# Leaving the second softmax of a gated slot attention undivided, and repairing it in the epsilon of the normalization

## The chip, the core and the metric

The kernel runs on one core of one Trainium2 chip. The metric is the device time of one execution in microseconds (us). A core has five engines that run their own instruction queues in order: PE (TensorE, matrix products; its weight loads are listed as PEld), DVE (VectorE), ACT (ScalarE), POOL (GpSimd) and SP (SyncE, which issues the DMAs). They wait for each other by semaphores.

## The reference

Input is x of 2 x 2048 x 512 in f32. One layer of gated slot attention with 16 heads, then a feed-forward layer with a Hadamard transform; each is followed by a residual sum and a layer norm. Of the attention, what matters here:

```
q, k (64 per head), v, g (128 per head), s (64 slots per head, clipped) = x @ weights
ok_t[m] = sum over u <= t of (q_t . k_u) * weight of token u in slot m      # M = 64 slots
p       = softmax(ok, over the 64 slots)
o_t     = sum over m of p_t[m] * (slot m's running mean of v up to t)
o       = o * rsqrt(mean(o*o over 128) + 1e-5) * g_norm_weight
o       = o * silu(g);   y = o @ Wo
```

The weights of the tokens in a slot are exp(s), divided by their running sum z. So ok is a causal product divided by z, and the same division by z is needed a second time when p meets the values.

If p is left as e = exp(ok - max), with S the sum of e over the slots, then o becomes S * o. The normalization gives the same result if its epsilon is multiplied by S*S, since S*o / sqrt(mean((S*o)^2) + S*S*eps) = o / sqrt(mean(o^2) + eps).

## The kernel before, in words

The heads go in four groups (g) of four; the 2048 tokens in 16 chunks (n) of 128, both batch rows at once. A `Step` is one group on one chunk: 64 steps, group by group. Its tiles hold the 128 tokens in the partitions and NQ = 4 pairs of columns of heads, eight (head, batch) pairs in all; `HALVES` are the two halves of 64 partitions, in which slots and state of two batch rows or heads lie.

`run` (called once per step) writes out by hand the order of the instructions of three steps in flight: `now` (projections, scores, the slots' softmax), `before` (the step one earlier: values, normalization, output products) and `old` (two earlier: the rest of the output products, rows stored). The order of PE, DVE, ACT and POOL is the order in which `run` calls the methods; nothing is moved by a scheduler there. DMAs are issued by SP.

All large products are made by seven products of quarter blocks (Strassen's scheme in Winograd's form): `q`, `v` and `o` with k = 1 to 7, whose sums lie in the PSUM tags c1 (two buffers), c2 and c3. `Unit.into` brings a product from PSUM to SBUF, on ACT (lines 458 and 460) or on DVE (463). PE's lines: 503 for q, k and s; 529 for values and gates; 746 for the output product, which reads the tile `ob`; its results are added to the rows on DVE (742).

The steps that the change and the prediction speak of, in the order of one `run`:

- PE's `state_values` (687) ends the values `po` of `before`. `gated` then squares them on ACT (704, three instructions because half of the partitions change sides), multiplies them by the gate on DVE (706), sums the squares on DVE (708), and on POOL scales and adds epsilon (710), raises to the power -0.5 (711) and multiplies (713).
- `softmax` of `now` on DVE: division by z (625), the maximum (631), its subtraction (633); the exponential on ACT (634).
- `softmax_sum`: sum over the slots (638) and its reciprocal (639) on DVE; the second multiplication by 1/z on POOL (640).
- `o_transposed` of `before`: eight transposes on PE (730) of what 713 made; `right_factor` copies them into `ob` on ACT (427, 428) and makes further parts on DVE (432, 433) and POOL (434, 435).
- `softmax_end` of `now`: the multiplication of r by 1/S on DVE (644).
- product 4 of `v`, copied by ACT (460); the tanh on ACT (539); products 1, 5 and 2 of `o` (746) with their additions (742) and, between them, the gate's last step on DVE (543). Then the next `run` begins with product 1 of `q` (503), product 3 of `o` and product 2 of `q`.
- r, made in this run, is read by the next run's `r_transposed` on PE (649), after product 6 of `q`.

The tile pool `small` has four buffers of each name, among them `sm`, which holds S.

```
do(now, "softmax_sum")
if o_last:
    nw["o"].sums(2)
    nw["o"].sums(3, nc.gpsimd)
do(before, "o_transposed")
do(now, "softmax_end")
main("v", 4)
```

Of the kernel before, what the change touches and what calls it, by code (L numbers as in the profile page):

```python
# [9 lines left out]
F32 = mybir.dt.float32  # L10
AF = mybir.ActivationFunctionType
ALU = mybir.AluOpType
AX = mybir.AxisListType
PSUM = bass.MemoryType.PSUM

P = 128
# [4 lines left out]
DV = 128  # L21
M = 64
HG = 4
NG = H // HG
NQ = 4
TH = P // 2
HALVES = (slice(0, TH), slice(TH, P))
# [6 lines left out]
EPS = 1e-5  # L34
# [4 lines left out]
def gated_slot_attention_ffn_kernel(  # L39
# [13 lines left out]
    nc = tc.nc  # L53
# [7 lines left out]
    small = ctx.enter_context(tc.tile_pool(name="small", bufs=4))  # L61
# [86 lines left out]
    xb, acc, res, h, wt = {}, {}, {}, {}, []  # L148
# [203 lines left out]
    with ExitStack() as att:  # L352
# [34 lines left out]

        QUARTERS = [(i, j, HALVES[j], s, HALVES[s], HALVES[s ^ j]) for i in range(NQ) for j in range(2) for s in range(2)]
        OPENS = (1, 2, 5)

        def settle(sums):

            nc.scalar.copy(small.tile([P, 1], F32, name="seen", bufs=1), sums)
# [71 lines left out]
        class Step:  # L465
# [31 lines left out]
            def multiply_q(self, out, k):  # L497
                wt = w["qks"].t
                for c in range(2):
                    xk, wk_ = self.xb[:, RIGHT[k], c, :], wt[:, LEFT[k], c, :]  # L500
                    for i in range(3):
                        a, b = (wk_[:, i * P : (i + 1) * P], xk) if i < 2 else (xk, wk_[:, 2 * P :])
                        nc.tensor.matmul(  # L503
                            out[:, i * P : (i + 1) * P], lhsT=a, rhs=b,
                            start=(k in OPENS and c == 0 and i == 0), stop=(c == 1), skip_group_check=True,
                        )
# [20 lines left out]
            def multiply_v(self, out, k):  # L527
                for c in range(2):
                    nc.tensor.matmul(  # L529
                        out, lhsT=self.xb[:, RIGHT[k], c, :], rhs=w["vg"].t[:, LEFT[k], c, :],  # L530
                        start=(k in OPENS and c == 0), stop=(c == 1), skip_group_check=True,
                    )
# [101 lines left out]
                nc.scalar.activation(r, r, AF.Exp, scale=DK**-0.5)  # L634

            def softmax_sum(self):
                self.sm = small.tile([P, 2 * NQ], F32, name="sm")
                nc.vector.tensor_reduce(self.sm, self.r8, AX.X, ALU.add)
                nc.vector.reciprocal(self.sm, self.sm)
                nc.gpsimd.tensor_tensor(self.r, self.r, self.iz, ALU.mult)  # L640

            def softmax_end(self):
                smb = self.sm.rearrange("p (h o) -> p h o", o=1).to_broadcast([P, 2 * NQ, M])
                nc.vector.tensor_tensor(self.r8, self.r8, smb, ALU.mult)


            def r_transposed(self):
# [48 lines left out]
            def gated(self):  # L696

                sq = c1.tile([P, 2, NQ, DV], F32, name="sq", tag="big")
                self.gj = self.t2[:, :, HD:].rearrange("p q (j d) -> p j q d", d=DV)

                every = slice(0, P)
                moves = [(0, every, every), (1, HALVES[0], HALVES[1]), (1, HALVES[1], HALVES[0])]
                for j, to, at in moves:
                    nc.scalar.activation(sq[to, j], self.po[j][at], AF.Square)  # L704
                for j, to, at in moves:
                    nc.vector.tensor_tensor(self.gj[to, j], self.po[j][at], self.gj[to, j], ALU.mult)  # L706
                ss = small.tile([P, 2 * NQ], F32, name="ss")
                nc.vector.tensor_reduce(ss, sq.rearrange("p j q d -> p (j q) d"), AX.X, ALU.add)  # L708
                self.state()
                nc.gpsimd.tensor_scalar(ss, ss, 1.0 / DV, EPS, ALU.mult, ALU.add)  # L710
                nc.gpsimd.tensor_tensor(ss, ss, mhalf, ALU.pow)
                ssb = ss.rearrange("p (j q o) -> p j q o", j=2, o=1).to_broadcast([P, 2, NQ, DV])
                nc.gpsimd.tensor_tensor(self.gj, self.gj, ssb, ALU.mult)
# [30 lines left out]
            def multiply_o(self, out, k):  # L744
                for c in range(2):
                    nc.tensor.matmul(  # L746
                        out, lhsT=self.ob[:, RIGHT[k], c, :], rhs=w["o"].t[:, LEFT[k], c, :],
                        start=(k in OPENS and c == 0), stop=(c == 1), skip_group_check=True,
                    )
# [248 lines left out]
        def run(new, now, before, old):  # L998


            def do(step, name, *args):
                if step is not None:
                    getattr(step, name)(*args)

            def main(name, k):

                if now is not None:
                    getattr(now, name)(k)
                elif before is not None:
                    for _ in range(FILL[name, k]):  # L1010
                        next(ups)
# [120 lines left out]
                nw["o"].sums(2)  # L1132
                nw["o"].sums(3, nc.gpsimd)
            do(before, "o_transposed")
            do(now, "softmax_end")
            main("v", 4)
            if last:
                nw["vg"] = load_vg(g + 1)
# [23 lines left out]
        with tc.manual_schedule(  # L1162
            engines={mybir.EngineType.PE, mybir.EngineType.DVE, mybir.EngineType.Activation, mybir.EngineType.Pool}
        ):
            steps[0].load_x()
            nw["qks"] = load_qks(0)
            steps[1].load_x()
            nw["vg"] = load_vg(0)
            nw["o"] = load_o(0)
            steps[0].make_x()  # L1170
            for k in range(4):
                nw["qks"].sums(k)
            N = len(steps)
            for i in range(N + 2):
                if i == N:
                    open_x("wvg", OUTER[3:], 4 * P)
                    open_acc("ux", tag="h1")
                    ups = up(0, h)
                run(*(steps[j] if 0 <= j < N else None for j in (i + 1, i, i - 1, i - 2)))
            for _ in pieces[0]:  # L1180
                pass
# [6 lines left out]
    with tc.manual_schedule(  # L1188
# [11 lines left out]
        for u in range(NU):  # L1200
            if u:
                h = {}
# [89 lines left out]
```

## Time and profile before

| | us |
|---|---|
| three runs | 3512.81, 3513.03, 3518.43; median 3513.03 |
| profiled execution, span from its first to its last instruction | 3516.1 (granted TensorE clock 0.999) |
| attention part, 0 to 2430 us: busy PE / DVE / ACT / POOL | 2388.6 / 1656.9 / 815.8 / 630.1 |
| rest, 2430 to 3516 us: busy PE / DVE / ACT / POOL | 1068.1 / 698.0 / 141.2 / 514.1 |
| line 639, 64 instructions on DVE | 13.0 (203 ns each) |
| line 644, 64 instructions on DVE | 77.9 (1217 ns each) |
| line 710, 64 instructions on POOL | 12.7 (198 ns each) |

The profile is of one execution; no time of its own is given for it beside its span, which is 3.1 us above the median of the three runs. A busy PE is not the same as PE at its peak, since the ends of matmuls are modelled; its starts are better guides. A line of the timeline gives start, length, engine, line of the code, what is written and read, and in brackets the idle time of that engine just before and who ended it.

### The profile page before, as it was taken

Reading aid. Unit: us, or ns where it says so; the run is one execution under the profiler, and the core shown is the slowest. Engines: PE = TensorE matmul, PEld = TensorE weight load, DVE = VectorE, ACT = ScalarE, POOL = GpSimd, SP = SyncE. Lnnn points to the kernel's source line nnn. Section 1 sums busy time; section 2 is a strip of 40 time slices with the busy share of each in tenths; the row PEclk is TensorE's granted clock in tenths of the full one; section 3 lists DMA queues with packets and bytes.
Section 4 is the critical chain, followed back from the end, with each engine's and each line's share of the span. In section 5 each row is a group of like instructions: output and inputs, shape, how many; then the busy total and the mean of one; then the engine's idle time right before and its main releaser. Section 6 shows DMA issues by size and latency. Waiting matters only on the chain. (4 is left out here: it accounts for less than half of the span.)

```text
span 3516.1 us, 75258 instructions
## 1 busy us (share of the span) xinstructions
PE 3456.7 (98%) x31840; PEld 2702.8 (77%) x31840; DVE 2354.9 (67%) x3940; ACT 957.0 (27%) x1712; POOL 1144.2 (33%) x1069
## 2 busy tenths in 40 slices
PE   8999999999999999999999999998999999999998
PEld 6777777677777677677777777776888888888887
DVE  5777776665666765656766677777666756756756
ACT  3333333333333333333333333332111111111110
POOL 1222223221221331221332222223634643643544
PEclk9999999999999999999999999999999999999999
DMA  5334334221122232122222243347555544445431
GB/s 184 118 113 138 118 119 152 93 72 62 55 66 70 94 96 65 52 66 70 74 99 68 69 140 129 102 160 270 171 179 205 174 161 176 156 151 184 163 135 68
DMA packets 208833, 425.03 MB, mean 121 GB/s; under 512 B 19696, under 2 KB 120432, under 8 KB 207472
## 3 DMA queue, kind: packets, MB, share of 16 engines
q1 hardware_dynamic: 208496, 420.22, 35.7%
q8 instruction: 250, 4.10, 0.5%
q14 instruction: 87, 0.71, 0.1%
HBM read 297.47 MB, written 125.30 MB: 120 GB/s over the span
## 5 line engine op out<-in xcount | busy, mean ns | idle before, releaser
L529 PE MATMUL c<-wvg,xb 128*128 128x512 f32 x1792 | 812.7, 598 | 4.0 <-DVE wvg L412 2.0
L529 PEld LDWEIGHTS c<-wvg,xb 128*128 128x128 f32 x1792 | 322.1, 190 | 369.6 <-issue 291.9
L503 PE MATMUL c<-xb,wqks 128*128 128x128 f32 x3584 | 553.2, 277 | 15.7 <-DMA wqks<-wqks_blocks 9.6
L503 PEld LDWEIGHTS c<-xb,wqks 128*128 128x128 f32 x3584 | 479.9, 193 | 43.7 <-DVE rows L742 21.5
L218 DVE TENSOR_TENSOR accux<-c,accux 128x512 f32<-128x512 f32 x496 | 341.4, 691 | 180.9 <-PE c L237 163.5
L276 PE MATMUL dc<-w2t,hid 128*128 128x256 f32 x1792 | 455.3, 379 | 2.1 <-DVE res L283 2.1
L237 PE MATMUL c<-wvg,xb 128*128 128x256 f32 x1792 | 432.0, 380 | 6.1 <-DVE accux L218 5.3
L742 DVE TENSOR_TENSOR rows<-c,rows 128x256 f32<-128x256 f32 x448 | 181.7, 418 | 335.9 <-PE c L746 331.4
L237 PEld LDWEIGHTS c<-wvg,xb 128*128 128x128 f32 x1792 | 338.8, 190 | 56.9 <-DVE accux L218 9.1
L276 PEld LDWEIGHTS dc<-w2t,hid 128*128 128x128 f32 x1792 | 340.2, 190 | 49.5 <-DVE res L283 3.3
L503 PE MATMUL c<-wqks,xb 128*128 128x128 f32 x1792 | 347.4, 276 | 0.0
L463 DVE TENSOR_TENSOR t<-c,kept 128x384 f32<-128x384 f32 (+1 forms) x384 | 230.6, 611 | 155.6 <-PE c L503 147.5
L237 PE MATMUL c<-wqks,xb 128*128 128x256 f32 x1344 | 325.1, 380 | 5.2 <-DVE accux L218 2.3
L458 ACT COPY kept<-c 128x384 f32<-128x384 f32 (+1 forms) x384 | 203.5, 530 | 457.8 <-PE c L503 369.5
L516 POOL TENSOR_TENSOR e<-e,zc 1x512 f32<-1x512 f32 x60 | 76.4, 1273 | 710.0 <-ACT e L515 710.0
L237 PEld LDWEIGHTS c<-wqks,xb 128*128 128x128 f32 x1344 | 253.9, 190 | 44.0 <-DVE accux L218 5.0
L503 PEld LDWEIGHTS c<-wqks,xb 128*128 128x128 f32 x1792 | 273.0, 193 | 0.0
L283 DVE TENSOR_TENSOR res<-dc,res 128x256 f32<-128x256 f32 x448 | 189.2, 423 | 117.9 <-PE dc L276 107.3
L573 DVE RECIPROCAL iz<-z 128x256 f32<-128x256 f32 x128 | 223.9, 1749 | 44.6 <-ACT z L564 44.6
L710 POOL TENSOR_SCALAR ss<-ss 128x8 f32<-128x8 f32 x64 | 12.7, 198 | 685.3 <-DVE ss L708 685.3
L706 DVE TENSOR_TENSOR t<-po,t 64x512 f32<-64x512 f32 (+1 forms) x192 | 131.6, 685 | 95.6 <-ACT sq L704 94.3
L252 POOL TENSOR_TENSOR accw<-accw,accux 128x512 f32<-128x512 f32 x64 | 80.8, 1276 | 275.7 <-DVE accux L218 274.3
(189 smaller groups left out, 4975.7 us busy)
## 6 DMA issues: line engine op xcount, KB each, us to landing
xb<-w13s SPq DMA_DIRECT2D x112, 896.0 KB
xb<-xd SPq DMA_DIRECT2D x48, 896.0 KB
yd<-rows SPq DMA_DIRECT2D x128, 256.0 KB
w2t<-w2s SPq DMA_DIRECT2D x32, 896.0 KB
rows<-yd SPq DMA_DIRECT2D x100, 256.0 KB
xd<-xb SPq DMA_DIRECT2D x16, 896.0 KB
wvg<-fxd SPq DMA_DIRECT2D x16, 896.0 KB
w13s<-inner SPq DMA_DIRECT2D x96, 128.0 KB
```

The costliest lines, as they stand in the source:

```text
L218: nc.vector.tensor_tensor(into[:, b], s, (into if first is None else first)[:, b], ALU.add)
L237: nc.tensor.matmul(s[:, j * TQ : (j + 1) * TQ], lhsT=w[:, LEFT[k], j, :], rhs=right[:, RIGHT[k], :], start=(k in (1, 2, 5) and j == 0), st ...
L252: (nc.gpsimd if u or m == 6 else nc.vector).tensor_tensor(o, o, t["u"][:, b], ALU.add)
L276: nc.tensor.matmul(s, lhsT=h["hid"][:, i, LEFT[m], k * P : (k + 1) * P], rhs=h["w2"][:, i, RIGHT[m], :], start=(m in (1, 2, 5) and i == 0) ...
L283: nc.vector.tensor_tensor(r, s, r, ALU.add)
L458: nc.scalar.copy(self.kept[k], s)
L463: nc.vector.tensor_tensor(t[:, to], s, self.kept[other], ALU.add)
L503: nc.tensor.matmul(out[:, i * P : (i + 1) * P], lhsT=a, rhs=b, start=(k in OPENS and c == 0 and i == 0), stop=(c == 1), skip_group_check=True,
L529: nc.tensor.matmul(out, lhsT=self.xb[:, RIGHT[k], c, :], rhs=w["vg"].t[:, LEFT[k], c, :], start=(k in OPENS and c == 0), stop=(c == 1), sk ...
L573: nc.vector.reciprocal(self.iz[:, h], self.z[:, h])
L706: nc.vector.tensor_tensor(self.gj[to, j], self.po[j][at], self.gj[to, j], ALU.mult)
L742: nc.vector.tensor_tensor(y_, self.uo.sum(k), y_, ALU.add)
```

## The change

The slots' exponentials are no longer divided by their sum. The reciprocal of the sum (639) and the multiplication `softmax_end` (644) leave DVE. In their place `softmax_sum` writes a tile `floor`, eps * S * S, by three ACT instructions (Square with the scale sqrt(eps)) that arrange S as `gated` needs it in the next run: [2, NQ] with the second half's partitions exchanged, by the same moves as the squares of the values, now named `MOVES`. In `gated` POOL's first operation adds 0 in place of epsilon, and one more POOL operation adds `floor`. The three ACT instructions stand in ACT's queue between the exponential and the copies of `right_factor`. The size of the scratch for software-made DMA descriptors is set to 2048.

```diff
+        MOVES = [(0, slice(0, P), slice(0, P)), (1, HALVES[0], HALVES[1]), (1, HALVES[1], HALVES[0])]
...
             def softmax_sum(self):
-                self.sm = small.tile([P, 2 * NQ], F32, name="sm")
-                nc.vector.tensor_reduce(self.sm, self.r8, AX.X, ALU.add)
-                nc.vector.reciprocal(self.sm, self.sm)
+                sm = small.tile([P, NQ, 2], F32, name="sm")
+                nc.vector.tensor_reduce(sm.rearrange("p q j -> p (q j)"), self.r8, AX.X, ALU.add)
                 nc.gpsimd.tensor_tensor(self.r, self.r, self.iz, ALU.mult)
 
-            def softmax_end(self):
-                smb = self.sm.rearrange("p (h o) -> p h o", o=1).to_broadcast([P, 2 * NQ, M])
-                nc.vector.tensor_tensor(self.r8, self.r8, smb, ALU.mult)
+                self.floor = small.tile([P, 2, NQ], F32, name="floor")
+                for j, to, at in MOVES:
+                    nc.scalar.activation(self.floor[to, j], sm[at, :, j], AF.Square, scale=EPS**0.5)
...
                 self.state()
-                nc.gpsimd.tensor_scalar(ss, ss, 1.0 / DV, EPS, ALU.mult, ALU.add)
+                nc.gpsimd.tensor_scalar(ss, ss, 1.0 / DV, 0.0, ALU.mult, ALU.add)
+                nc.gpsimd.tensor_tensor(ss, ss, self.floor.rearrange("p j q -> p (j q)"), ALU.add)
                 nc.gpsimd.tensor_tensor(ss, ss, mhalf, ALU.pow)
...
             do(before, "o_transposed")
-            do(now, "softmax_end")
             main("v", 4)
...
-    nc = bacc.Bacc("TRN2", target_bir_lowering=False, num_devices=1)
+    nc = bacc.Bacc("TRN2", target_bir_lowering=False, num_devices=1, dynamic_dma_scratch_size=2048)
```

More of the change, by code (lines that the diff above doesn't have):

```diff
@@ L699, in gated @@
                 self.gj = self.t2[:, :, HD:].rearrange("p q (j d) -> p j q d", d=DV)
-                every = slice(0, P)
-                moves = [(0, every, every), (1, HALVES[0], HALVES[1]), (1, HALVES[1], HALVES[0])]
-                for j, to, at in moves:
+                for j, to, at in MOVES:
                     nc.scalar.activation(sq[to, j], self.po[j][at], AF.Square)
-                for j, to, at in moves:
+                for j, to, at in MOVES:
                     nc.vector.tensor_tensor(self.gj[to, j], self.po[j][at], self.gj[to, j], ALU.mult)
```

## The prediction

> **What bounds the kernel now.** I read the page's shares first, then the table of waits, then the timeline of one step (38 us, of 64) engine by engine. Columns of the shares: busy time, share of the span, instructions.
>
> ```profile
> PE 3456.7 (98%) x31840; PEld 2702.8 (77%) x31840; DVE 2354.9 (67%) x3940; ACT 957.0 (27%) x1712; POOL 1144.2 (33%) x1069
> ```
>
> TensorE (PE) is busy in 98% of the span; ACT and POOL have room on average. So whatever takes work off DVE can win only what PE now waits for, and whatever makes PE wait is lost in full. The table of waits (engine, line, what it waited for: total us, times, longest) tells where PE's weight loads (PEld) stop in the 64 steps:
>
> ```profile
> PEld c L746 <- ACT ob L427: 47.8, 64, 2.1
> ...
> PEld ps L730 <- POOL t L713: 37.9, 64, 0.8
> DVE r L644 <- POOL r L640: 36.8, 64, 1.2
> ...
> PEld c L503 <- DVE rows L742: 21.5, 43, 1.6
> ```
>
> Twice in every step PE's next load is released by another engine: by POOL before the transposes of L730, and by ACT's copy L427 before the output products of L746. The timeline of a middle step (start us, us, engine and line, idle before) shows how tight that is. PE and its loads:
>
> ```profile
> 477.70 1.07 PE L730 MATMUL ps<-ident,t 128*128 128x128 f32 x8
> 478.62 1.88 PE L529 MATMUL c<-wvg,xb 128*128 128x512 f32 x4
> 480.34 2.86 PE L746 MATMUL c<-wo__224,ob 128*128 128x256 f32 x12
> ...
> 480.33 2.46 PEld L746 LDWEIGHTS c<-wo__224,ob 128*128 128x128 f32 x12 [0.67 <-ACT ob L427]
> ```
>
> The load of L746 starts 0.05 us after L427 ends (479.72 + 0.57 = 480.29), and L746's first matmul follows the last L529 by 0.43 us, the usual interval of an L529. PE loses almost nothing there today, and has no slack either. ACT's queue around it, and the squares of L704 (three instructions, 128, 64 and 64 partitions):
>
> ```profile
> 479.18 0.63 ACT L634 ACTIVATE r<-r 128x512 f32<-128x512 f32 x1 [5.84 <-DVE r L633]
> 479.72 0.57 ACT L427 COPY ob<-ps 128x512 f32<-128x512 f32 x1
> 480.18 0.38 ACT L428 COPY ob<-ps 128x256 f32<-128x256 f32 x1
> ...
> 469.15 1.82 ACT L704 ACTIVATE sq<-po 128x512 f32<-128x512 f32 x3 [1.22 <-PE po L687]
> ```
>
> L427 runs right behind the exponential; what sets it is the exponential's place. And that is set by DVE's chain, back to back from L706 on, which starts when PE has ended L687:
>
> ```profile
> 478.39 0.69 DVE L633 TENSOR_TENSOR r<-r,mx 128x512 f32<-128x512 f32 x1
> 479.00 0.68 DVE L463 TENSOR_TENSOR t<-c,kept 128x512 f32<-128x512 f32 x1
> 479.84 0.69 DVE L638 TENSOR_REDUCE sm<-r 128x8 f32<-128x512 f32 x1 [0.16 <-ACT r L634]
> 480.56 0.20 DVE L639 RECIPROCAL sm<-sm 128x8 f32<-128x8 f32 x1
> ...
> 481.99 1.20 DVE L644 TENSOR_TENSOR r<-r,sm 128x512 f32<-128x512 f32 x1 [0.56 <-POOL r L640]
> 483.11 0.74 DVE L742 TENSOR_TENSOR rows<-c,rows 128x256 f32<-128x256 f32 x2
> 483.77 1.21 DVE L543 SCALAR_TENSOR_TENSOR t<-th,t 128x1024 f32<-128x1024 f32 x1
> 484.91 0.95 DVE L742 TENSOR_TENSOR rows<-c,rows 128x256 f32<-128x256 f32 x2
> ```
>
> Both removed instructions, L639 and L644, stand behind the exponential. They delay the row additions L742, which free the PSUM bank that a q product (L503) needs.
>
> **The change part by part.**
>
> Removed from DVE: 64 x (0.203 + 1.217) = 91 us of work, and the 36.8 us in which L644 waited for POOL. Almost all is hidden behind PE. What PE gets back is its wait before L503: from its start times, intervals longer than usual by 0.14 us in most steps, and by 0.4 to 1.3 us in eight; 42 cases, 11.2 us in all. Intervals of this sort inside L746 (DVE is late with another part of ob) add 1.9 us in 5 cases. Gain: 0 to 13 us. I take 13, for PE also comes later to this place (next part), so that the wait goes altogether.
>
> Added to ACT: three squares, in the queue between the exponential L634 and the copy L427, waiting for DVE's sum L638. This is a new wait, and L427, L428, L460 and the tanh queue behind it; PE's L746 waits for L427. Per step:
> - L638 ends at 479.84 + 0.69 = 480.53, L427 starts today at 479.72: 0.81 us (the same in 61 steps of 63; 1.16 and 2.09 in the last two, together 1.6 more).
> - from DVE's end to ACT's start: 0.09 us (L633 ends 479.09, L634 starts 479.18).
> - three squares of 128x4, 64x4 and 64x4. One costs between 0.16 us (the 128x1 copy, L393) and 0.21 us: an ACT instruction on 1024 columns took 1.058 and one on 512 took 0.632, so 0.206 is left without columns. Neighbours overlap by 0.095 us (L634 and L427) or not at all: the three squares of L704, the same shapes in partitions, started 0.62 and 0.61 apart and took 0.60 each. So three cost 3 x (0.16 - 0.095) = 0.20 at least and 3 x 0.21 + 0.09 of gaps = 0.72 at most. I take 0.60, near the row of L704, which is nearest in kind.
> - sum: 0.81 + 0.09 + 0.60 = 1.50 us, between 1.10 and 1.62.
>
> PE has nothing else to do there (it goes in order), so all of it is a stall before L746. It can happen in 63 steps (the first run has no output product): 63 x 1.50 + 1.6 = 96 us, between 71 and 104.
>
> The Trainium skill, "ScalarE: Activation LUTs", section "What ACT_TABLE_LOAD costs", gives an ACTIVATE with immediate operands 186 ns plus 0.833 ns per column and an overlap of about 93 ns between neighbours. By that the squares cost 3 x (0.189 - 0.093) = 0.29 us and the stall is 1.19 us a step, 77 us in all; L704's starts don't show the overlap, and the measurement decides for the higher price.
>
> POOL, new addition of 128x8 in front of the power: 0.198 (L710, same size) + 0.083 between neighbours = 0.28 us on the chain L708, L710, L711, L713, L730. In 48 steps PE takes L730 as soon as L713 ends, so L730 comes up to 0.28 later; in the last dozen there are 0.29 us of slack. But the exponential depends on L687, not on L730, so this moves PE only within the 1.50 us that it must wait at L746 anyway. I take 0; if it were not covered, 50 x 0.28 = 14 us. Below zero it can't be: nothing leaves POOL.
>
> Costed at nothing: POOL's multiplication L640, now the last on r: it ends at 481.95, and its reader on PE, the transposes L649 of the next run, starts at 490.36; the 8.4 us between hid L644 too, so r being ready 1.2 us earlier wins nothing either. The Square table: L704 squares between exponential and tanh, and the table of groups has one table load for the whole attention part (L458) and one for the rest (L193), so none is added. The smaller DMA scratch: the queues listed are hardware and instruction queues only, no transfer goes through it. SP's queue keeps its order. The feed-forward part (1086 us from 2430 on) is untouched.
>
> Sum: +96 - 13 = +83 us. The profiled execution spans 3516.1 us, 3.1 above the median of 3513.03 and below the highest of the three times, 3518.43 (which would leave 2.4 around it). The difference of 0.1% is far below the sum; on the median: 3596 us.
>
> **Rivals.**
>
> 1. The squares overlap like L634 and L427 and are short: 1.10 us a step, 71 - 13 = +58, 3571 us. The same mechanism at its low end. At its high end with nothing recovered: +104, 3617 us.
>
> 2. Faster: ACT's new wait is covered and only DVE's relief is left, -13 us, 3500 us. For it: PE's matmuls (not the loads) wait for L427 only 8 times, 5.0 us in all, and ACT is busy 27%. Against it: the load of L746 starts 0.05 us after L427 in the step shown, and in all 64 steps it is released by it. It decides where the stall is below 13 / 63 = 0.2 us a step, that is, if L427 could come 1.3 us later unnoticed.
>
> 3. The addition on POOL is not absorbed, because ACT's work before the exponential gets tied to PE's transposes: +14 us more, 3610 us. Against: nothing between L687 and L634 reads what L730 writes.
>
> 4. A table load at each change of function, 1.283 us as in the two there are, 128 times: +164 us more, 3760. Against it is the single load in the attention part with Square, Exp and Tanh in one loop.
>
> **How the numbers follow.** The likeliest, with its two ends 3571 to 3617, has 0.82; rival 3 has 0.08; rival 2 0.06 (with 0.02 more for no change, if the stall and the relief cancel); rival 4 and other losses 0.02. Less than 0.2% (7 us) from no change is about what a measurement of this kernel can't tell. So faster 0.06, same 0.02, slower 0.92. Range: 3567 to 3618, which holds the likeliest and most of rival 3.
>
> **What would show it.** Right: in the table of waits the load of L746 waits for ACT's L427 (L428 of the new file) for some 140 us instead of 47.8, and PE's matmuls show 1.2 us of idle time before each L746; ACT shows three small squares after the exponential with an idle time ahead of them, released by the sum on DVE; the waits of L503 for DVE's rows are almost gone; PE's share falls towards 96%. POOL's wait before L730 grows by 0.25 us a step without lengthening the step further. Wrong: L746 flows on without a gap (rival 2), or steps grow by more than 1.7 us, or table loads appear. A step that grows by less than 0.9 us would say that the squares overlap with something I took as strictly ordered.

## The result

The changed kernel takes 3608.62 us (median; 3601.97 to 3610.45) beside 3514.53 us for the kernel before: ratio 1.0257, 95% interval 1.0242 to 1.0271. It is slower by 94 us; 83 had been forecast, and the time lies inside the range of 3567 to 3618. The profiled execution spans 3608.7 us, 92.6 more than that of before.

The shares of the page after the change:

```profile
PE 3469.8 (96%) x31840; PEld 2711.1 (75%) x31840; DVE 2282.9 (63%) x3812; ACT 999.1 (28%) x1904; POOL 1136.8 (32%) x1133
```

DVE lost 72 us of busy time, ACT gained 42, and the span grew: work moved from an engine that had cover to a place that had none. The table of waits (engine, line, what was waited for: total us, times, longest) says which place; lines of the new file are one or two off those of before (745 is the output product, 428 ACT's copy, 729 the transposes, 644 the new squares):

```profile
PEld c L745 <- ACT ob L428: 133.8, 64, 4.8
...
PE c L745 <- ACT ob L428: 81.4, 63, 4.0
...
PEld ps L729 <- POOL t L712: 56.2, 64, 1.2
...
ACT floor L644 <- DVE sm L639: 49.8, 64, 2.0
```

The loads of the output product waited 47.8 us before and wait 133.8 now, and PE's matmuls themselves stand 81.4 us, 1.3 us in every step, where the table of before has

```profile
PE c L746 <- ACT ob L427: 5.0, 8, 1.3
```

The wait of the q products (now L504) for DVE's row additions, 21.5 us in 43 cases before, is down to one case of 0.2 us. A middle step, on ACT and then on PE:

```profile
493.46 0.63 ACT L635 ACTIVATE r<-r 128x512 f32<-128x512 f32 x1 [5.84 <-DVE r L634]
494.84 0.64 ACT L644 ACTIVATE floor<-sm 128x4 f32<-128x4 f32 x3 [0.75 <-DVE sm L639]
495.50 0.59 ACT L428 COPY ob<-ps 128x512 f32<-128x512 f32 x1
```

```profile
493.17 1.88 PE L530 MATMUL c<-wvg,xb 128*128 128x512 f32 x4
496.14 2.86 PE L745 MATMUL c<-wo__224,ob 128*128 128x256 f32 x12 [1.08 <-ACT ob L428]
```

ACT's copy starts 2.04 us after the exponential (493.46 to 495.50) instead of 0.54, and PE's first output product starts when that copy is done. On DVE the step now shows room where the division was, and a wait for ACT in front of its part of ob:

```profile
494.12 0.69 DVE L639 TENSOR_REDUCE sm<-r 128x8 f32<-128x512 f32 x1 [0.15 <-ACT r L635]
496.45 0.42 DVE L433 TENSOR_TENSOR ob<-ps,ob 128x256 f32<-128x256 f32 x1 [1.65 <-ACT ob L429]
```

Step by step, from PE's start times at the first transposes of each step, the commonest growth is 1.35 us (36.75 to 38.10, some 20 steps); the steps in which PE had no wait before q to recover mostly grew by 1.60 (37.61 to 39.20).

### The profile page after: what moved, and what is told of

It is laid out like the page before. It is cut to its first block, busy times and chain, and to the rows that moved or that the text cites. A ratio compares the mean times of both kernels' runs of the same rounds, so it can differ in the third digit from the quotient of the medians.

```text
span 3608.7 us, 75391 instructions
## 1 busy us (share of the span) xinstructions
PE 3469.8 (96%) x31840; PEld 2711.1 (75%) x31840; DVE 2282.9 (63%) x3812; ACT 999.1 (28%) x1904; POOL 1136.8 (32%) x1133
## 5 line engine op out<-in xcount | busy, mean ns | idle before, releaser
L504 PE MATMUL c<-xb,wqks 128*128 128x128 f32 x3584 | 548.1, 276 | 11.0 <-DMA wqks<-wqks_blocks 9.1
L504 PEld LDWEIGHTS c<-xb,wqks 128*128 128x128 f32 x3584 | 482.8, 192 | 25.4 <-issue 18.6
L741 DVE TENSOR_TENSOR rows<-c,rows 128x256 f32<-128x256 f32 x448 | 189.9, 424 | 438.6 <-PE c L745 434.1
L504 PE MATMUL c<-wqks,xb 128*128 128x128 f32 x1792 | 346.9, 275 | 0.0
L504 PEld LDWEIGHTS c<-wqks,xb 128*128 128x128 f32 x1792 | 272.6, 192 | 0.0
L704 DVE TENSOR_TENSOR t<-po,t 64x512 f32<-64x512 f32 (+1 forms) x192 | 131.6, 685 | 96.7 <-ACT sq L702 95.4
```

The source lines that it names most:

```text
L504: nc.tensor.matmul(out[:, i * P : (i + 1) * P], lhsT=a, rhs=b, start=(k in OPENS and c == 0 and i == 0), stop=(c == 1), skip_group_check=True,
L741: nc.vector.tensor_tensor(y_, self.uo.sum(k), y_, ALU.add)
```

## The experiments

The theory: three small instructions that wait, in the middle of ACT's queue, cost PE a stall of 1.5 us a step; POOL's extra addition is covered by that stall; DVE's relief is worth some 13 us where the stall is not. The rivals: the squares cost by their mere work wherever they stand; POOL's addition costs beside the stall; DVE's relief is hidden behind PE.

**1. The squares moved behind the tanh.** A method of its own, called one place later, where ACT is idle:

```diff
+                self.sm = sm
+            def softmax_floor(self):
                 self.floor = small.tile([P, 2, NQ], F32, name="floor")
                 for j, to, at in MOVES:
-                    nc.scalar.activation(self.floor[to, j], sm[at, :, j], AF.Square, scale=EPS**0.5)
+                    nc.scalar.activation(self.floor[to, j], self.sm[at, :, j], AF.Square, scale=EPS**0.5)
...
             do(now, "tanh")
+            do(now, "softmax_floor")
```

> The three squares stand behind the tanh in ACT's queue, where ACT is idle for 2.4 us; everything else as in the changed kernel. Theory (place in ACT's queue): the stall of 1.5 us before the output products is gone and with it the cover over POOL's addition, 0.27 us before the transposes in 48 steps, +13 us; DVE's relief is worth some -15 us. So about the time of before, 3512 us, between 3500 and 3522. Rival (the three squares cost ACT time that PE pays for wherever they stand): 63 x 0.65 = 41 us above before, 3555 us or more.

Measured: 3516.59 us beside 3518.58 of before; ratio 0.9993 (0.9983 to 1.0002). The whole loss is gone, with the same instructions on every engine. The timeline of ACT shows them between the tanh and the next copy, which still waits for PE:

```profile
780.35 1.06 ACT L540 ACTIVATE th<-t 128x1024 f32<-128x1024 f32 x1
781.31 0.62 ACT L646 ACTIVATE floor<-sm 128x4 f32<-128x4 f32 x3
783.66 0.48 ACT L459 COPY kept<-c 128x384 f32<-128x384 f32 x1 [1.73 <-PE c L504]
```

The rival that prices the squares by their work (3555 us) falls. What the steps gain from DVE's relief they give back before the transposes, where POOL's addition is no longer covered by a stall:

```profile
PEld ps L731 <- POOL t L714: 56.6, 64, 1.3
...
PEld c L747 <- ACT ob L428: 35.5, 64, 2.1
```

By PE's start times the intervals before L731 are longer by 14.3 us in all than in the kernel before; some 3 us of it come back in shorter intervals inside the output product.

**2. The squares moved, and POOL's chain as short as before.** The factor 1/DV goes into the scale of ACT's squares of the values, so that POOL's first operation is the addition of `floor`:

```diff
-                    nc.scalar.activation(sq[to, j], self.po[j][at], AF.Square)
+                    nc.scalar.activation(sq[to, j], self.po[j][at], AF.Square, scale=DV**-0.5)
...
-                nc.gpsimd.tensor_scalar(ss, ss, 1.0 / DV, 0.0, ALU.mult, ALU.add)
                 nc.gpsimd.tensor_tensor(ss, ss, self.floor.rearrange("p j q -> p (j q)"), ALU.add)
```

> As the kernel with the late squares, and 1/DV goes into the scale of the squares of the values, so that POOL has as many instructions on the chain to the transposes as before. Theory: only DVE's relief is left, -13 to -17 us, 3498 us, faster than before; the wait of PE's transposes for POOL is that of before (0.6 us a step). Rival (PE is the bound and the relief was hidden): 3514 us.

Measured: 3505.65 us beside 3518.58; ratio 0.9962 (0.9947 to 0.9977). This version is faster than the kernel before, by 0.4%, and so than the changed one. The wait at the transposes is back at its old size, and the wait of the q products for DVE has nearly gone:

```profile
PEld c L746 <- ACT ob L428: 48.1, 64, 2.1
...
PEld ps L730 <- POOL t L713: 36.2, 63, 0.7
...
PEld c L504 <- DVE rows L742: 2.7, 4, 0.7
```

It also settles the price of POOL's addition where nothing covers it: beside it the two kernels differ only in the scale of ACT's squares, and their ratios by 0.0031, some 11 us (14.4 in the intervals before the transposes, less the 3 us that come back).

**3. POOL's chain shortened with the squares left in the change's place.** The edit is the second half of experiment 2 alone.

> The changed kernel with POOL's extra instruction taken away (1/DV in the scale of the squares of the values), the squares of the sums where the change puts them. Theory: POOL's addition is covered by the stall, so nothing changes: 3608 us, within 4. PE waits 0.27 us less at the transposes and as much more before the output products. Rival (the addition costs beside the stall): 13 us less, 3595 us.

Measured: 3604.92 us, ratio 1.0241 (1.0224 to 1.0258) beside the changed kernel's 1.0257 (1.0242 to 1.0271). The intervals overlap; the spans differ by 2.3 us (3606.4 and 3608.7). PE's wait only moved from the transposes to the output product:

```profile
PEld c L744 <- ACT ob L428: 146.7, 64, 4.8
...
PE c L744 <- ACT ob L428: 94.3, 63, 4.0
...
PEld ps L728 <- POOL t L711: 36.3, 63, 0.6
```

By PE's start times the intervals before the product are longer by 12.9 us than in the changed kernel (in the table 94.3 against 81.4), and those before the transposes shorter by 13.9 (the waits of the loads there: 36.3 against 56.2). So the same addition is worth 11 us in experiment 1 and nothing to speak of here: a cost on a path that is not the longest.

**4. The squares alone, added to the kernel before.** The sum goes into a tile of its own, the reciprocal and the multiplication stay on DVE, and `floor` is written where the change writes it but not used:

```diff
-                self.sm = small.tile([P, 2 * NQ], F32, name="sm")
-                nc.vector.tensor_reduce(self.sm, self.r8, AX.X, ALU.add)
-                nc.vector.reciprocal(self.sm, self.sm)
+                sm = small.tile([P, NQ, 2], F32, name="sum")
+                nc.vector.tensor_reduce(sm.rearrange("p q j -> p (q j)"), self.r8, AX.X, ALU.add)
+                self.sm = small.tile([P, 2 * NQ], F32, name="sm")
+                nc.vector.reciprocal(self.sm, sm.rearrange("p q j -> p (q j)"))
                 nc.gpsimd.tensor_tensor(self.r, self.r, self.iz, ALU.mult)
+                self.floor = small.tile([P, 2, NQ], F32, name="floor")
+                for j, to, at in MOVES:
+                    nc.scalar.activation(self.floor[to, j], sm[at, :, j], AF.Square, scale=EPS**0.5)
```

> The kernel before plus the three squares alone, in the place that the change gives them; their result is not used, and the division stays on DVE. Theory: the stall makes PE late for L503's wait on the rows anyway, so nearly the whole loss is here without the relief: 3605 us, between 3598 and 3615. Rival (DVE's relief is worth its 13 us beside the stall): 3620 us or more.

Measured: 3603.24 us, ratio 1.0239 (1.0224 to 1.0255). The three squares alone make the whole loss, and the division, still on DVE, costs nothing beside them: PE comes so late to the q products that DVE's rows are there (two waits are left, 1.0 us in all). The smaller DMA scratch is in this kernel too, and in experiment 1, which loses nothing by it.

This kernel's steps are even 0.08 us shorter than those of the changed kernel in most cases (+1.27 against +1.35). The traces show where most of that lies: PE's transposes of e (L555, in the new files L556) wait for DVE's second mask of scores (L661; L667 here), and wait longer where the division is gone. Before, in the changed kernel and here:

```profile
PEld ps L555 <- DVE a L661: 19.5, 63, 0.3
...
PEld ps L556 <- DVE a L661: 23.5, 63, 0.4
...
PEld ps L556 <- DVE a L667: 19.1, 62, 0.3
```

PE's interval there (from its start times) is 0.41 us instead of 0.34 in most steps of every kernel without the division (the changed one and experiments 1, 2, 3, 5, 6 and 7), 4.0 us in all. In the traces of the changed kernel and of experiment 5, DVE's first mask of scores (584; 585 in the changed file) waits for POOL beside PE, with a semaphore instruction of its own ahead of it, in 63 of 64 steps, and in a middle step it starts 0.07 us later; with the division (before, and here) that is so in one step only. The first mask is written into a buffer of r's (both have the tag "r"), which DVE wrote last with the division and POOL writes last without it.

**5. The division taken away, nothing added.** The reciprocal and `softmax_end` are removed from the kernel before; the epsilon is left as it was.

```diff
-                nc.vector.reciprocal(self.sm, self.sm)
...
-            do(now, "softmax_end")
```

> The kernel before without the reciprocal and the multiplication on DVE; nothing is added, so the epsilon is not scaled by the squared sum and this part of the computation is left out. Theory: PE's wait for the rows before L503 goes, -13 us with a possible 2 more, 3500 us. Rival (hidden behind PE): 3514 us.

Measured: 3505.03 us beside 3516.95; ratio 0.9967 (0.9954 to 0.9980). DVE's relief is worth 12 us where PE is on time, commonly 0.18 us a step in the first 50 and nothing in the later ones, whose q products did not wait. Experiment 2, which computes all of the reference, gets the same.

**6. The same squares without the wait.** They read the maximum, which DVE finished before the exponential began:

```diff
+                self.mx = mx
...
-                    nc.scalar.activation(self.floor[to, j], sm[at, :, j], AF.Square, scale=EPS**0.5)
+                    nc.scalar.activation(self.floor[to, j], self.mx.rearrange("p (q j) -> p q j", j=2)[at, :, j], AF.Square, scale=EPS**0.5)
```

> The changed kernel, but the three squares read the maximum, which is there before the exponential, in place of the sum: the same instructions in the same place without the wait on DVE (the epsilon is scaled by another number than the reference's). Theory: the wait is 0.81 + 0.03 us of the 1.51 us and the squares 0.66; so L427 comes 0.7 us later than before, 63 x 0.7 = 44 us less 13 of recovered waits: 3545 us, between 3535 and 3560. If the wait alone makes the stall: 3505 us. If the squares alone do: 3608 us.

Measured: 3545.95 us beside 3516.95; ratio 1.0080 (1.0065 to 1.0095). Work and wait share the stall as expected. ACT's queue in a step:

```profile
786.79 0.63 ACT L636 ACTIVATE r<-r 128x512 f32<-128x512 f32 x1 [5.84 <-DVE r L634]
787.33 0.62 ACT L645 ACTIVATE floor<-mx 128x4 f32<-128x4 f32 x3
787.98 0.59 ACT L428 COPY ob<-ps 128x512 f32<-128x512 f32 x1
```

The copy starts 1.18 us after the exponential: 0.54 is the old distance, 0.64 the three squares. In the changed kernel it is 2.04; the other 0.86 is the wait.

**7. The squares made twice.** The loop of the three squares is repeated in its place.

> The changed kernel with the three squares made twice. Theory: they follow each other without overlap, 0.215 us each, and every one is a stall of PE: 63 x 0.65 = 41 us more, 3650 us. If they overlapped by 0.09 us each, 24 us more, 3632 us. If ACT had slack there: 3608 us. The longer stalls may also bring more stretches of 3.4 us at half of the granted clock, of which the profile of the changed kernel has five and that of before none inside its span: up to 1.7 us each.

Measured: 3669.86 us, ratio 1.0433 (1.0416 to 1.0451); its span is 59.2 us above that of the changed kernel, not 41. The squares follow each other without overlap, and the copy comes behind the sixth:

```profile
427.19 0.66 ACT L644 ACTIVATE floor<-sm 128x4 f32<-128x4 f32 x3 [0.75 <-DVE sm L639]
427.88 0.66 ACT L646 ACTIVATE floor<-sm 128x4 f32<-128x4 f32 x3
428.56 0.58 ACT L428 COPY ob<-ps 128x512 f32<-128x512 f32 x1
```

Three more squares are 0.69 us (427.19 to 427.88), 43 us in 63 steps; PE's intervals before the output product grew by 44.3. Most of the rest came from the clock: 13 stretches at half of the granted clock (three of them 6.8 us, the others 3.4), against five in the changed kernel, not counting one in the first 40 us and one at the very end, which every profile has. PE's matmuls that start inside these stretches are later by 20 us in all than in the kernel before, in the changed kernel by 7, and an ordinary step with such a stretch is longer by 1.68 us (3.98 against 2.30 above the kernel before).

## Why the prediction was right

*The place.* The step named, ACT's new wait ahead of the copy that PE's output product needs, is the one that decides: moving the squares away from it removes the loss (experiment 1), adding them alone to the kernel before makes it (4).

*The size per step.* Forecast 0.81 + 0.09 + 0.60 = 1.50 us. Measured in the step shown: from the old start of the copy to the end of the sum 0.81; from DVE's end to the first square 0.03 (494.805 to 494.838, unrounded); three squares up to the copy's start 0.66; together 1.50. The semaphore was overestimated by 0.06 and the squares underestimated by as much; that these two cancel was luck. The choice between 0.20 and 0.72 for the squares, made by the three squares of L704, was the one that mattered. The squares in the new trace are 0.20 to 0.21 us long, with gaps of 0.01 us between them and 0.02 before the copy.

The Trainium skill, "ScalarE: Activation LUTs", section "What ACT_TABLE_LOAD costs", has 186 ns plus 0.833 ns per column and an overlap of about 93 ns between neighbours. The length is near to it (0.187 to 0.208 us here, in the changed kernel and experiments 1 and 6). The overlap is seen between the exponential and the first square of experiment 6 (0.095 us) but not between the squares; the measurement decides, and by the page the stall would have been 0.3 us a step too small.

*POOL's addition.* Forecast: 0.28 us on its chain, covered. It took 0.20 us and 0.08 between neighbours; the waits of PE's loads before the transposes rose by 18.3 us and PE's own intervals there by 13.9, but taking the addition away (experiment 3) shortened the span by only 2.3. Where the cover is gone it costs 11 us (experiment 1), for which 14 had been named as the uncovered price.

*The relief.* Forecast 13 us. The excess of PE's intervals before the q products fell by 10.9 us, and that of the second interval after such a wait by 4.5. The number was nearly right, but it was booked as a gain of the removed division, with PE's lateness as what completes it. For the changed kernel the lateness is enough: experiment 4 has the same gain with the division in place. The removed division is worth 12 us only where there is no stall (5). Beside the stall it costs some 4 us, in the wait of the transposes of e (4). The prediction put the new order of the writers of r at nothing, having looked at r's next reader and not at the next writer of its buffer.

*The sum.* PE's intervals before the output product grew by 85.0 us, those before the transposes of L730 by 13.9: 98.9, where 96 was forecast. 15.4 come back, where 13 was forecast. Two terms were not forecast: 4.0 us before the transposes of e, and the five stretches at half clock, in which PE's matmuls lost 6.7 (some 1.6 in each of four, 0.3 in the fifth, which fell on a wait). That is 94 us, beside 92.6 of the spans; the rest is spread over many small intervals. The forecast of 83 was short by about these two terms.

*The rivals.* Rival 1's ends (3571 and 3617) enclose the result; rival 2 asked for a stall below 0.2 us, and it is 1.5; rival 3 falls with experiment 3; of rival 4 nothing is seen, since the squares follow the exponential and precede the tanh without any table load between them.

## What to carry to other kernels

An instruction that is small and waits belongs where its engine is idle, not where its input is born: 0.6 us of work and 0.9 us of wait cost 90 us in one place of ACT's queue and nothing four instructions further on. Before taking work off an engine, look for what released the bound engine's next instruction with no slack, here two waits that the share of busy time (98%) did not show as a loss; a new step on the longer chain is paid in full, and one on the shorter chain only once the longer one is repaired. When two costs lie in one step, remove them one at a time and together: the same addition on POOL was worth some 2 us (by the spans) or 11, the same relief nothing or 12. When an engine no longer is the last to write a buffer, look at who writes the buffer next, and not only at who reads it: here one more semaphore wait on DVE cost 4 us.

## What the runs showed of the hardware that was not expected

The clock of PE fell to half for stretches of 3.4 us after waits much shorter than that. In the changed kernel, around the output product of the step with a long stall (stretch: length, busy us of PE, PEld, DVE, ACT, POOL with instructions, then the granted clock of PE, the share of the DMA engines and GB/s):

```profile
609.00:613.10 4.10, 1.87 (x7) 0.98 (x6) 2.26 (x5) 2.95 (x8) 3.39 (x3) 1.00 0.25 76
613.10:616.50 3.40, 3.40 (x11) 2.69 (x10) 2.15 (x4) 0.70 (x1) 1.53 (x3) 0.50 1.01 378
616.50:620.00 3.50, 3.50 (x29) 3.40 (x29) 1.46 (x3) 0.48 (x1) 3.50 (x2) 1.00 0.98 395
```

And in the kernel with six squares, in one of its last steps, where PE's interval before the output product is mostly 2.59 us (0.43 before the change):

```profile
2415.00:2418.50 3.50, 1.51 (x6) 0.63 (x5) 1.05 (x3) 2.60 (x10) 1.26 (x1) 1.00 0.39 109
2418.50:2422.00 3.50, 3.50 (x10) 2.79 (x9) 1.66 (x5) 1.23 (x2) 1.45 (x2) 0.51 0.39 158
```

The stretches begin on a fixed grid: two starts in the changed kernel, 613.12 and 1855.57 us, are 364 times 3.413 us apart. I laid that grid over all nine profiles and summed PE's idle time, by the profile's spans, in each of its windows from 40 us on. In the windows right before a half-clock stretch began PE was idle for 1.8 us or more of the 3.4; in the windows that no such stretch followed it was idle for 1.8 us at most, but for three of 1.88 to 1.97. The kernel with six squares shows both: the stalls of its ordinary steps, with 1.8 us of idle time, brought no such stretch. Of twelve stalls in its last steps, with 1.95 to 2.0 us, the seven that lay wholly inside one window were each followed by one; the five that were split over two windows were not. A whole window of idleness is not needed. Why some stretches last 6.8 us has not been followed. The price is 1.7 us in an ordinary step, which a forecast of long stalls has to add; together it was 7 us here and some 20 with six squares, since stretches that fall on other waits cost less.
